# A four-layer graph network on one core: layer rows turned through DRAM in 128-byte pieces, PSUM banks 2/2/4, residual sums in two pieces, and another planned order

## The chip, the cores and the metric

The kernel runs on one core of a Trainium2 chip. The metric is the device time of one execution in microseconds (us), from start to end of the program. A core has five engines with queues of their own: PE (TensorE, matrix products), DVE (VectorE), ACT (ScalarE), POOL (GpSimd) and SP (SyncE, which issues nearly all DMAs here). PE writes only to PSUM, a memory of eight banks of 512 fp32 numbers per partition; DVE and ACT empty the banks.

## The reference, cut to what matters

The input is x, 128 graphs of 64 nodes with 256 features, and an integer adjacency matrix per graph. Four layers follow each other; each normalizes the rows, cuts negatives to zero, computes something over the graph, and adds it to x (the residual sum).

```
h = maximum(layernorm(x), 0);  x = x + elu(attention_4_heads(h, adj))
h = maximum(layernorm(x), 0);  x = x + elu(attention_1_head(h, adj))
h = maximum(layernorm(x), 0);  x = x + relu(relational_conv(h, adj))
h = maximum(layernorm(x), 0);  x = x + gru_3_steps(h, adj)
# one gru step:  m = h @ weight[i];  a = A^T @ m;  h = gru_cell(a, h)
```

All is fp32. An adjacency entry above 1 or very large attention scores would take a general path that is built into the program and is skipped for these inputs.

## The kernel before, in words

**Tiling.** The 8192 rows are cut into 16 groups of 512 rows (`G` = 4 tiles of 128 partitions). Each group passes layer 0, layer 1, layer 2 (called "the layers" here) and then three recurrent steps. A step is 42 matrix products of 256 columns (six sets of seven products in a scheme that saves one product in eight; the sums of weights are prepared in `wsum`, the sums of states on POOL in `hS` and `aS`). The steps of two neighbouring groups are interleaved: (1,0), (0,2), (1,1), (2,0), ... The layers of later groups are filled in between.

**Rows to columns.** A layer needs its normalized rows `hn` turned, with features on the partitions (`hT`), because PE contracts over partitions. For groups from 2 on `layernorm_T_by_dma` does this without PE. ACT writes `hn`; DVE turns 32x32 blocks into `tb` (same buffers as `hn`); one DMA writes all of `tb` to the DRAM tile `way`, in pieces of 4 KB; four DMAs read it back into `land`, in pieces of 1 KB; two ACT copies `hT<-hn` (the profile calls `land` by its buffer, `hn`) bring the pieces into the order that the products want. The recurrence turns its rows in a like manner (`way<-tb`, then `hnat<-way` or `hT<-way`), and is not changed.

**PSUM.** `Banks.room` splits the eight banks: three for `mt` (shared by all tiles of the layers and of the adjacency products, `mm`, `mn`, `tp`, `tq`), two for `sy` and three for `sz`, which take the products of the recurrent steps. A tile takes a free bank of its kind; its first product waits until the last reader of the bank's former tile is done.

**Small products.** `along` (states times adjacency), `aggregate_graphs` and the last product of layer 2 use 64x64 quarters of PE. `beside` (line 842) issues each such block of products as one unit, so no other product stands inside it. There are 130 such blocks.

**Residual sums.** `elu_add` (layers 0 and 1, from group 1 on) and `Recurrence.finish` add a group's result to `xg` in one POOL instruction over 128x1024 numbers.

**Who sets the order.** No engine's order follows the source. Every call is recorded as an `Op`; `Plan.emit` then simulates the engines with estimated durations (`cost`, `port`), 40 times forward and backward from a random start (`SEED`), takes the best ranks, shifts the jobs' due times by a fixed list of pseudo-random moves (`MOVES`), and emits all instructions in the resulting order, engine by engine. All instructions so emitted carry line 550 in the profile, so tiles tell them apart. In the first 115 us, where the plan sees PE idle, it puts in products of a constant (`warm`, line 1664; into an `sz` bank, read by nobody).

```
PASSES, SEED, SPREAD = 40, 35, 50.0
ISSUE, TURN = 665.0, 197.0
took -= self.TURN if op.parts and parts else 0.0     # one small block right after another
```

Of the kernel before, what the change touches and what calls it, by code (L numbers as in the profile page):

```python
# [10 lines left out]
F32 = mybir.dt.float32  # L11
# [6 lines left out]
S = 32  # L18
# [204 lines left out]
class Plan:  # L223
# [30 lines left out]
    def note(self, engine, call, cost, writes, reads, after=(), port=0.0, dma=False):  # L254
# [23 lines left out]
            b.ops.append(op)  # L278
        return op

    PASSES, SEED, SPREAD = 40, 35, 50.0
    MOVES = (
        10, 23, 28, 30, 40, 45, 69, 85, 99, 108, 114, 116, 126, 132, 141, 159, 210, 227, 236, 241, 319, 326, 339, 343,
        354, 365, 383, 426, 448, 489, 544, 596, 636, 646, 651, 652, 704, 736, 741, 742, 743, 752, 760, 807, 869, 944,
        951, 987, 991, 1089, 1101, 1110, 1124, 1248, 1251, 1273, 1452, 1492, 1498, 1501, 1678, 1834, 1893, 1966, 2005,
        2010, 2196, 2270, 2336, 2377, 2433, 2441, 2584, 2658, 2695, 2697, 2873, 3006, 3016, 3031, 3058, 3081, 3167,
        3224, 3271, 3376, 3444, 3459, 3524, 3571, 3664, 3704, 3719, 3750, 3772, 3786, 3953, 4165, 4169, 4192, 4344,
        4481, 4581, 4610, 4913, 4970, 5115, 5123, 5266, 5287, 5433, 5732, 6133, 6139, 6156, 6871, 6933, 7088, 7813,
        7842, 8883, 9045, 9231, 9268, 10172, 10189, 10284, 10634, 10814, 10991, 13029, 13068, 13352, 13896, 14140,
        16577, 16772, 17027, 533, 1980, 2724, 3643, 4767, 7708,  # L290
    )
    LEEWAY = {"PE": 100.0, "DVE": 100.0, "Activation": 100.0, "Pool": 100.0, "SP": 300.0, "-": 0.0}
    OVERLAP = {"DVE": 83.0, "Activation": 95.0, "Pool": 43.0}
# [318 lines left out]
def kernel(  # L612
# [122 lines left out]
    def layernorm_T_by_dma(work, dram, src, hT, natural=None):  # L735


        n = src.shape[1]
        st = work.tile([P, n, 6], F32, name="st")
        mv = work.tile([P, n, 2], F32, name="mv")  # L740
        for p in range(n):
            nc.vector.bn_stats(st[:, p, :], src[:, p, :])
            nc.vector.bn_aggr(mv[:, p, :], st[:, p, :])
        var = work.tile([P, n], F32, name="var")
        rstd = work.tile([P, n], F32, name="rstd")
        nm = work.tile([P, n], F32, name="nm")
        nc.scalar.activation(var, mv[:, :, 1], AF.Identity, bias=eps)
        nc.scalar.mul(nm, mv[:, :, 0], -1.0)
        nc.gpsimd.tensor_tensor(rstd, var, mhalf[:, :n], ALU.pow)
        nc.gpsimd.tensor_tensor(nm, nm, rstd, ALU.mult)  # L750
        hn = work.tile([P, n, D], F32, name="hn") if natural is None else natural
        for p in range(n):
            to, of = hn[:, p], src[:, p, :]
            if natural is not None:
                to, of = spread(hn[:, :, p : p + 1]), of.rearrange("p (k i b) -> p k i b", k=K, b=S)
            nc.scalar.activation(to, of, AF.Relu, bias=nm[:, p : p + 1], scale=rstd[:, p : p + 1])
        if natural is not None and hT.shape[1] == K:
            tb = work.tile([P, K, n, P], F32, name="tb")
            for k in range(K):
                nc.vector.transpose(  # L760
                    tb[:, k].rearrange("p n (j b) -> p n j b", b=S),
                    hn[:, :, :, k * S : (k + 1) * S].rearrange("p j n b -> p n j b"),
                )
            for i in range(P // S):
                for j in range(P // S):
                    to = hT[j * S : (j + 1) * S].rearrange("p k n (i c) -> p (k n) i c", c=S)[:, :, i]
                    of = tb[i * S : (i + 1) * S].rearrange("p k n q -> p (k n) q")
                    nc.sync.dma_start(to, of[:, :, j * S : (j + 1) * S])
            return
        if natural is not None:  # L770
            tb = work.tile([P, P // S, K, n, S], F32, name="tb")
            for k in range(K):
                nc.vector.transpose(
                    tb[:, :, k].rearrange("p j n c -> p n j c"),
                    hn[:, :, :, k * S : (k + 1) * S].rearrange("p j n b -> p n j b"),
                )
            way = dram.tile([P, P // S, K * n * S], F32, name="way")
            nc.sync.dma_start(way, tb.rearrange("p j k n c -> p j (k n c)"))
            for j in range(P // S):
                nc.sync.dma_start(  # L780
                    hT[j * S : (j + 1) * S].rearrange("p i k x -> p i (k x)"),
                    way[:, j].rearrange("(i b) x -> b i x", b=S),
                )
            return
        tb = work.tile([P, P // S, K, n, S], F32, name="tb")
        nc.vector.transpose(
            tb.rearrange("p j k n c -> p n k j c"), hn.rearrange("p n (k j b) -> p n k j b", k=K, b=S)
        )
        way = dram.tile([P, P // S, K * n * S], F32, name="way")
        nc.sync.dma_start(way, tb.rearrange("p j k n c -> p j (k n c)"))  # L790
        land = work.tile([P, P // S, K * n, S], F32, name="land")
        for j in range(P // S):
            nc.sync.dma_start(
                land[j * S : (j + 1) * S].rearrange("p i x c -> p i (x c)"),
                way[:, j].rearrange("(i b) x -> b i x", b=S),
            )
        for a in range(2):
            nc.scalar.copy(
                hT[:, a].rearrange("p k n (e c) -> p (k n) e c", c=S),
                land[:, 2 * a : 2 * a + 2].rearrange("p e x c -> p x e c"),  # L800
            )

    def transpose_blocks(psum, dst, src, rblocks, scale=1.0, turned=False):
# [46 lines left out]
    def elu_add(work, src, o, engine, by_scalar=False):  # L850

        em = work.tile(list(o.shape), F32, name="em")
        if by_scalar:
            nc.scalar.activation(em, o, AF.Relu, scale=-1.0)
            nc.scalar.activation(em, em, AF.Exp, scale=-1.0)
        else:
            nc.vector.tensor_scalar(em, o, 0.0, None, op0=ALU.min)
            nc.scalar.activation(em, em, AF.Exp)
        nc.vector.scalar_tensor_tensor(em, em, -1.0, o, op0=ALU.add, op1=ALU.max)
        engine.tensor_tensor(src, src, em, ALU.add)  # L860

    def block_diagonal(dst, src, scalar, op):

# [116 lines left out]
    class Recurrence:  # L980
# [72 lines left out]

        def finish(self):

            to = self.src.rearrange("p n (k i b) -> p (n k) i b", k=K, b=S)
            nc.gpsimd.tensor_tensor(to, to, spread(self.hnat), ALU.add)
            self.store(self.src, slice(None))

        def step(self, i, back=True, in_parts=False):  # L1060
# [159 lines left out]
    with ExitStack() as s1:  # L1220
# [4 lines left out]
        class Banks(Pool):  # L1225
# [4 lines left out]
            early = psum = spare = True  # L1230

            def room(self, tag, base):
                return {"mt": 3, "sy": 2, "sz": 3}.get(tag, 1)


            def tile(self, shape, dtype, name, **kwargs):
# [31 lines left out]
        class Layer:  # L1268

            place = {"em": "hn", "dg": "hn", "tb": "hn", "land": "hn"}

            shared = {"hn": 3, "o": 2, "st": 4, "mv": 4, "var": 4, "rstd": 4, "nm": 4, "rec": 4}

# [384 lines left out]
        if 115.0:  # L1660
            warm = const.tile([P, P], F32, name="warm")
            nc.nc.vector.memset(warm, 1.0)
            pause = psum.real.tile([P, P], F32, name="sz", tag="sz", bufs=3)
            nc.spare = lambda: psum.spare and nc.nc.tensor.matmul(pause, warm, warm, start=True, stop=True)  # L1664
        with tc.manual_schedule(engines={getattr(mybir.EngineType, e) for e in ENGINES.values()}):
            nc.emit()
# [215 lines left out]
```

## Time and profile before

| | us |
|---|---|
| three runs | 1311.43, 1312.52, 1318.44 (median 1312.52) |
| profiled execution, device time | 1311.0 |
| its span, first to last instruction | 1309.2 |
| PE busy | 1288.8 (98% of the span) |
| DVE, ACT, POOL busy | 1052.5, 857.7, 700.3 |
| mean busy share of the 16 DMA engines | 35% |
| granted PE clock | 0.997 of full |

The profiled execution is 1.5 us below the median. Outside its span lie 1.8 us. A busy PE is not a full one: matrix products are pipelined, their records overlap and their ends are modelled, so a short wait can hide within "busy". Where it matters, the distance of two starts in the timeline is read instead. In a row of a group, "out<-in" are the program's tiles, then partitions x elements; for a product the stationary operand's name may stand first.

### The profile page before, as it was taken

The page shows a single profiled execution, that of the slowest core. Times are in us where ns is not written, and L with a number is a line of the kernel's source. Part 1 is how long each engine was busy: PE and PEld are TensorE (multiplying, and loading weights), DVE is VectorE, ACT ScalarE, POOL GpSimd, SP SyncE. Part 2 cuts the span into 40 slices and gives each one's busy share as a digit, 9 for nine tenths or more (in the row PEclk, how much of TensorE's full clock was granted, in tenths as well). Part 3 has the DMA queues.
Part 4 walks back from the last instruction along what each step waited for, and adds up shares of the span by engine and source line. Part 5 has one row for each costly group of instructions (what it writes and reads, how often), then busy time and mean ns, then how long its engine had stood idle before and what let it go on. Part 6 is the DMA issues. An engine that isn't in the chain of part 4 may idle for free.

```text
span 1309.2 us, 27708 instructions
## 1 busy us (share of the span) xinstructions
PE 1288.8 (98%) x9761; PEld 1024.4 (78%) x9761; DVE 1052.5 (80%) x2532; ACT 857.7 (66%) x2179; POOL 700.3 (53%) x859
## 2 busy tenths in 40 slices
PE   9999999999999999999999999999999999999996
PEld 8667877788777887777787787778878787778885
DVE  7887788968879798887968879796969877776665
ACT  7876666766667676666657657766766667655543
POOL 4845454645555473655527456373747556435443
PEclk9999999999999999999999999999999999999998
DMA  8202133343343434334333444433334433322112
GB/s 249 87 19 63 33 118 106 112 128 118 118 125 111 141 98 135 131 104 122 128 112 114 121 136 122 130 130 102 118 98 138 146 86 117 104 77 71 60 65 69
DMA packets 139349, 142.64 MB, mean 109 GB/s; under 512 B 46912, under 2 KB 126272, under 8 KB 139200
## 3 DMA queue, kind: packets, MB, share of 16 engines
q1 hardware_dynamic: 137856, 140.50, 35.1%
q8 instruction: 80, 1.31, 0.4%
q14 instruction: 69, 0.57, 0.1%
q10 hardware_dynamic: 1344, 0.27, 0.1%
HBM read 78.39 MB, written 61.80 MB: 107 GB/s over the span
## 4 chain that ended last, share of the span: by engine, by line
PE 86%; DVE 6%; POOL 3%; ACT 3%; issue 1%; DMA 1%; SPq 0%; DVEq 0%; ACTq 0%; POOLq 0%
PE sy L550 35%; PE sz L550 26%; PE mm L550 16%; PE mm L842 3%; PE tp L842 3%; DVE hT L550 2%; DVE t L550 1%; PE tp L550 1%; POOL rstd L550 1%; ACT hn L550 1%; PE sz L1664 1%; PE tq L842 1%; POOL xg L550 1%; DVE r L550 1%; DMA t<-row 1%
## 5 line engine op out<-in xcount | busy, mean ns | idle before, releaser
L550 POOL TENSOR_TENSOR r<-hT,hT 128x256 f32<-128x256 f32 x192 | 154.4, 811 | 237.7 <-ACT hT L550 236.9
L550 DVE SCALAR_TENSOR_TENSOR hT<-r,hT 128x256 f32<-128x256 f32 (+1 forms) x290 | 186.4, 647 | 27.1 <-ACT r L550 24.7
L550 PE MATMUL sy<-aS,wsum 128*128 128x256 f32 x576 | 172.8, 384 | 1.9 <-DVE hT L550 1.9
L550 PE MATMUL sy<-hS,wsum 128*128 128x256 f32 x576 | 171.2, 383 | 2.0 <-ACT z L550 1.5
L550 PE MATMUL sz<-hS,whh 128*128 128x256 f32 x576 | 171.4, 383 | 0.6 <-DVE z L550 0.5
L550 PE MATMUL sz<-aS,wc 128*128 128x256 f32 x576 | 164.9, 382 | 0.9 <-DVE hT L550 0.9
L550 DVE TENSOR_TENSOR hT<-hT,sz 128x256 f32<-128x256 f32 x288 | 117.7, 410 | 42.6 <-PE sz L550 38.9
L550 ACT ACTIVATE hT<-hT,bi 128x256 f32<-128x256 f32 x192 | 95.8, 504 | 51.8 <-DVE hT L550 51.3
L550 PEld LDWEIGHTS sy<-hS,wsum 128*128 128x128 f32 x576 | 107.1, 190 | 27.8 <-issue 5.9
L550 POOL TENSOR_TENSOR rstd<-var,mhalf 128x4 f32<-128x4 f32 (+1 forms) x70 | 76.7, 1095 | 97.2 <-ACT var L550 92.5
L550 PEld LDWEIGHTS sy<-aS,wsum 128*128 128x128 f32 x576 | 107.2, 190 | 25.1 <-issue 6.0
L550 PEld LDWEIGHTS sz<-aS,wc 128*128 128x128 f32 x576 | 108.2, 190 | 21.6 <-issue 5.8
L550 PEld LDWEIGHTS sz<-hS,whh 128*128 128x128 f32 x576 | 107.5, 190 | 21.9 <-issue 5.9
L550 ACT ACTIVATE hT<-sy,bh 128x256 f32<-128x256 f32 x192 | 90.0, 469 | 49.8 <-PE sy L550 48.6
L550 POOL TENSOR_TENSOR aS<-aT 128x256 f32<-128x256 f32 x96 | 79.0, 823 | 81.6 <-ACT aT L550 78.8
L550 PE MATMUL mm<-wl,hT 128*128 128x512 f32 x248 | 118.9, 595 | 1.3 <-DVE u L550 1.0
L550 ACT ACTIVATE hn<-xg,nm,rstd 128x256 f32<-128x256 f32 x200 | 109.4, 594 | 15.1 <-POOL nm L550 11.9
L550 ACT COPY z<-sy 128x256 f32<-128x256 f32 x192 | 70.2, 369 | 66.8 <-PE sy L550 65.2
L550 DVE TENSOR_TENSOR hT<-hT,sy 128x256 f32<-128x256 f32 x192 | 79.2, 412 | 37.5 <-PE sy L550 35.1
L550 DVE TENSOR_TENSOR z<-sz,z 128x256 f32<-128x256 f32 x192 | 79.6, 416 | 25.7 <-PE sz L550 23.4
L550 DVE BATCH_NORM_STATS2 st<-xg 128x6 f32<-128x256 f32 x256 | 95.6, 406 | 5.1 <-DMA xg<-in_x_dram 3.1
L550 POOL TENSOR_TENSOR hS<-hT 128x256 f32<-128x256 f32 x96 | 81.8, 852 | 24.5 <-DVE hT L550 15.2
(212 smaller groups left out, 3197.9 us busy)
## 6 DMA issues: line engine op xcount, KB each, us to landing
way<-tb SPq DMA_DIRECT2D x59, 512.0 KB, 2.7
hnat<-way SPq DMA_DIRECT2D x184, 128.0 KB, 3.0
way<-hn SPq DMA_DIRECT2D x42, 512.0 KB, 3.0
hn<-way SPq DMA_DIRECT2D x168, 128.0 KB, 2.9
xg<-in_x_dram SPq DMA_DIRECT2D x15, 512.0 KB, 4.3
out_dram<-xg SPq DMA_DIRECT2D x15, 512.0 KB, 3.0
t<-row SPq DMA_DIRECT2D x28, 256.0 KB, 4.0
hT<-way SPq DMA_DIRECT2D x52, 128.0 KB, 2.9
```

The costliest lines, as they stand in the source:

```text
L550: return do(*[real(a) for a in args], **{k: real(v) for k, v in kwargs.items()})
L842: nc.nc.tensor.matmul(*[real(x) for x in product], start=True, stop=True)
L1664: nc.spare = lambda: psum.spare and nc.nc.tensor.matmul(pause, warm, warm, start=True, stop=True)
```

## The change

Five edits, in one diff:

1. **Turned rows.** `way` and `land` are replaced by a DRAM tile `fine`. Four DMAs write `tb` (one for each 32 partitions, pieces of 1 KB), and two DMAs, one for each half `e`, read 256 KB each straight into `hT`, in 128-byte pieces. The two ACT copies are gone, and `land` no longer takes an `hn` buffer. This is done 42 times.
2. **Banks.** `mt` 3 to 4, `sz` 3 to 2, `sy` stays 2.
3. **`elu_add`** adds in two instructions over half the tiles each.
4. **`finish`** likewise.
5. **`SEED` 35 to 36 and a new list `MOVES`**: all engines' orders change.

```
-    PASSES, SEED, SPREAD = 40, 35, 50.0
+    PASSES, SEED, SPREAD = 40, 36, 50.0
     MOVES = (
-        10, 23, 28, 30, 40, 45, 69, 85, 99, 108, 114, 116, 126, 132, 141, 159, 210, 227, 236, 241, 319, 326, 339, 343,
...
+        4, 9, 10, 16, 23, 24, 27, 52, 54, 69, 126, 127, 131, 135, 153, 160, 168, 195, 197, 225, 228, 230, 231, 238,
...
     )
...
-        way = dram.tile([P, P // S, K * n * S], F32, name="way")
-        nc.sync.dma_start(way, tb.rearrange("p j k n c -> p j (k n c)"))
-        land = work.tile([P, P // S, K * n, S], F32, name="land")
-        for j in range(P // S):
+        fine = dram.tile([2, P // S, S, 2, K * n * S], F32, name="fine")
+        for i in range(P // S):
             nc.sync.dma_start(
-                land[j * S : (j + 1) * S].rearrange("p i x c -> p i (x c)"),
-                way[:, j].rearrange("(i b) x -> b i x", b=S),
+                fine[i % 2, :, :, i // 2].rearrange("j b x -> b j x"),
+                tb[i * S : (i + 1) * S].rearrange("p j k n c -> p j (k n c)"),
             )
-        for a in range(2):
-            nc.scalar.copy(
-                hT[:, a].rearrange("p k n (e c) -> p (k n) e c", c=S),
-                land[:, 2 * a : 2 * a + 2].rearrange("p e x c -> p x e c"),
+        for e in range(2):
+            nc.sync.dma_start(
+                hT.rearrange("p a k n (e c) -> p (a k n) e c", c=S)[:, :, e],
+                fine[e].rearrange("j b a (x c) -> (j b) (a x) c", c=S),
             )
...
-        engine.tensor_tensor(src, src, em, ALU.add)
+        n = src.shape[1]
+        m = max(1, n // 2)
+        for p in range(0, n, m):
+            engine.tensor_tensor(src[:, p : p + m], src[:, p : p + m], em[:, p : p + m], ALU.add)
...
-            to = self.src.rearrange("p n (k i b) -> p (n k) i b", k=K, b=S)
-            nc.gpsimd.tensor_tensor(to, to, spread(self.hnat), ALU.add)
+            m = G // 2
+            for p in range(0, G, m):
+                to = self.src[:, p : p + m].rearrange("p n (k i b) -> p (n k) i b", k=K, b=S)
+                nc.gpsimd.tensor_tensor(to, to, spread(self.hnat[:, :, p : p + m]), ALU.add)
...
-                return {"mt": 3, "sy": 2, "sz": 3}.get(tag, 1)
+                return {"mt": 4, "sy": 2, "sz": 2}.get(tag, 1)
...
-            place = {"em": "hn", "dg": "hn", "tb": "hn", "land": "hn"}
+            place = {"em": "hn", "dg": "hn", "tb": "hn"}
...
-            pause = psum.real.tile([P, P], F32, name="sz", tag="sz", bufs=3)
+            pause = psum.real.tile([P, P], F32, name="sz", tag="sz", bufs=2)
```

## The prediction

> **What bounds the kernel now.** I read the page's busy shares first, then its chain of waits, then PE's timeline, measuring each wait as the distance between starts less the products' own time.
>
> ```profile
> PE 1288.8 (98%) x9761; PEld 1024.4 (78%) x9761; DVE 1052.5 (80%) x2532; ACT 857.7 (66%) x2179; POOL 700.3 (53%) x859
> ...
> PE 86%; DVE 6%; POOL 3%; ACT 3%; issue 1%; DMA 1%; SPq 0%; DVEq 0%; ACTq 0%; POOLq 0%
> ```
>
> PE sets the end: nothing else is near 98%, and the chain is 86% PE. No edit removes a needed product, so only what keeps PE from its products can change. By the timeline (a 256-column product starts 0.43 us after the one before) that is:
> - start-up, to 95 us: 11 gaps over 0.25 us, 5.9 us in all, beside 48 `warm` products of 0.22 us (10.5 us);
> - 95 to 1250 us: nine gaps, 8.9 us in all: 0.43 (at 217), 0.89 (220), 1.64 (386), 1.82 (526), 1.38 (600), 1.18 (639), 0.42 (1027), 0.44 (1111), 0.68 (1140);
> - the end, from 1290 us: six gaps, 4.5 us, and 7.7 us from the last product to the end of the output DMA;
> - the edges of 130 small blocks.
>
> The edges, in PE's timeline (start, duration, operation):
>
> ```profile
> 631.91 0.59 PE L550 MATMUL sy<-hS,wsum 128*128 128x256 f32 x2
> 632.44 0.27 PE L842 MATMUL tp<-abd,hnat 64*64 64x64 f32 x2
> 632.45 0.27 PE L842 MATMUL tq<-abd,hnat 64*64 64x64 f32 x2
> 632.54 0.23 PE L842 MATMUL tp<-abd,hnat 64*64 64x64 f32 x2
> ...
> 633.38 0.23 PE L842 MATMUL tq<-abd,hnat 64*64 64x64 f32 x2
> 633.53 0.70 PE L550 MATMUL sy<-aS,wsum 128*128 128x256 f32 x2
> ```
>
> The large product ends its turn at 632.34 and the next starts at 633.53: 1.19 us. Inside, 16 rounds follow each other by 0.058 us: 0.93 us. So 0.26 us of a block is edge.
>
> The largest kind of gap, in the timeline of all engines:
>
> ```profile
> 383.75 2.80 POOL L550 TENSOR_TENSOR xg<-xg,hn 128x1024 f32<-128x1024 f32 x1
> ...
> 384.60 2.50 DVE L550 SCALAR_TENSOR_TENSOR hT<-r,hT 128x512 f32<-128x512 f32 x1
> ...
> 385.83 0.59 PE L550 MATMUL sz<-hS,whh 128*128 128x256 f32 x2
> ...
> 387.20 0.37 ACT L550 COPY r<-sy 128x256 f32<-128x256 f32 x1 [1.99 <-DVE hT L550]
> ...
> 387.47 0.38 ACT L550 COPY z<-sy 128x256 f32<-128x256 f32 x1
> ...
> 387.90 0.70 PE L550 MATMUL sy<-hS,wsum 128*128 128x256 f32 x2 [1.48 <-ACT z L550]
> ```
>
> A POOL residual sum runs; the DVE operation beside it, about 0.7 us otherwise, ends only 0.6 us after POOL does; ACT waits for DVE, so empties an `sy` bank late; PE waits 1.64 us for the bank. The gaps at 217, 220 and 526 fall beside a residual sum in the same way, and the one at 639 behind a DVE operation that waited for it: 5.96 of the 8.9 us.
>
> **What the Trainium skill says.**
> - *SBUF — State Buffer*, "Who interferes with whom": a DVE instruction with two SBUF inputs and a GpSimd instruction that reads SBUF exclude each other for a whole instruction. The trace agrees: 2.50 us above.
> - *TensorEngine Tiling (Array Packing)*, "Key Properties": changing the tiling mode drains TensorE. The trace agrees: 0.26 us a block.
> - *DMA: Bandwidth & Descriptors*, "Why small descriptors are slow (HBM only)": each packet has a fixed overhead. The trace before has no 128-byte reads from DRAM; its nearest rows are below.
>
> **The change part by part.** Beside durations I use the instruction order of the two built programs.
>
> *Order on PE.* Before, each of the 130 small blocks stands alone. After, 97 do, 15 pairs and one triple follow each other directly: 113 runs, 17 fewer pairs of edges. No adjacent blocks are in the trace, so a join saves between 0 and 0.24 us; I take 0.20, as both blocks use the same quarters: 17 x 0.20 = **-3.4** (0 to -4.1).
>
> *Start-up.* 35 `warm` products instead of 48; 72.3 us of other products stand ahead of the first recurrent one in both. 13 x 0.22 = 2.8 us less filler, which ends PE sooner only where what PE then needs is there: I take half, **-1.4** (-5 to +3; the start-up's order is new, and DVE is busy in all of 20 to 40 us).
>
> *Residual sums.* The tile's durations:
>
> ```profile
> L550 POOL TENSOR_TENSOR xg<-xg,hn x32: 1269/2360/2806, 42.9 to 1130.1; 128x1024 f32<-128x1024 f32 x28, 128x512 f32<-128x512 f32 x4
> ```
>
> 47 become 94 (28 and 15 of 1024 numbers become halves of 1.27 us, four of 512 become quarters); 43 x (2 x 1.27 - 2.36) = 8 us more on POOL, covered by its 47% idle. The longest block on DVE falls by 1.09 us: the gaps beside residual sums shrink from 0.43, 0.89, 1.64, 1.82, 1.18 to 0, 0, 0.55, 0.73, 0.09: -4.6 us, if DVE gets in between the halves. Group 0's four sums on DVE become eight.
>
> *Banks.* I summed the products' times between the last product into a tile and the first product of the tile that takes its bank (oldest first). An emptying needs about 0.9 us, so below 1.35 us there is little to spare. Such reuses: before 11 (`mt`), 55 (`sy`), 7 (`sz`); after 0, 60, 46. Six of the nine gaps stand before a product into an `sy` bank: 5.9 us for 55 tight reuses. With halves 3.3 of that goes; 2.6 stays. After has 106 tight reuses of `sy` and `sz`: 2.6 x 106/55 = 5.0 us. The three gaps of layer products (1.38, 1.18, 0.42) become about 1.5. Steady part together: 5.0 + 1.5 - 8.9 = **-2.4** (-7 to +6).
>
> *Turned rows.* ACT loses 84 copies:
>
> ```profile
> L550 ACT COPY hT<-hn 128x512 f32<-128x512 f32 x84 | 49.3, 613 | 5.4 <-DMA hn<-way 4.9 <-issue 0.5
> ```
>
> 49.3 us of an engine at 66%: off PE's path but for the gap of 0.68 us at 1140, where a copy stood behind long ACT work. I count nothing. The DMAs (tile, count, KB each, us to landing), then two stretches whose last columns are DMA share and GB/s:
>
> ```profile
> way<-hn SPq DMA_DIRECT2D x42, 512.0 KB, 3.0
> ...
> hn<-way SPq DMA_DIRECT2D x168, 128.0 KB, 2.9
> ...
> hT<-tb SPq DMA_DIRECT2D x16, 32.0 KB, 2.0
> ```
>
> ```profile
> 1184.00:1194.00 10.00, 10.00 (x48) 8.81 (x47) 5.84 (x14) 4.23 (x10) 0.69 (x2) 1.00 0.28 43
> ```
>
> ```profile
> 349.60:353.00 3.40, 3.40 (x18) 2.97 (x17) 3.38 (x11) 3.12 (x8) 2.74 (x4) 1.00 0.13 29
> ```
>
> The first holds the 16 `hT<-tb` alone, 4096 packets of 128 bytes between SBUF tiles: 0.28 x 10 x 16 / 4096 = 11 ns each. The second holds four `eg` loads, 384 packets of 256 bytes from DRAM and few others: 0.132 x 3.4 x 16 / 438 = 16 ns. A new read has 2048 packets over 16 engines: 128 x 11 to 16 ns = 1.4 to 2.1 us. 84 of them are 118 to 176 us of all engines; the writes and reads they replace nearly cancel (same bytes), so the share goes from 35% to 44-48%: no bound. Path before: write 3.0, issue of four reads 4 x 0.43, landing 2.9, two copies 1.2 = 8.8 us. After: four writes 1.7, landing 2.9, two reads issued at 0.61 each, data 2 x (1.4 to 2.1), about 2 fixed = 10.6 to 12.0, less whatever the issues overlap: 0 to 3 us later. SP issues 252 DMAs instead of 210: 42 x (4 x 0.43 + 2 x 0.61 - 0.34 - 4 x 0.43) = 37 us more of a mostly waiting queue; behind a read that waits for its four writes stand `row<-fT`, `t<-row` and `way<-tb` of the recurrence. Before, PE waits for such rows once (0.42 us at 1027), so most of the delay is covered by the lead of the layers; I take **+0.7** (-0.4 to +20).
>
> *The end.* 19.8 us of products stand after the last adjacency block instead of 17.2, and the first of them to use its result comes 3.4 us after it instead of 1.7: **0** (-1.7 to +1.5).
>
> Sum: -3.4 - 1.4 - 2.4 + 0.7 = -6.5 us on 1311.0: 1304.5 for a profiled execution; the median stood 1.5 above it: **1306.0**.
>
> **The rivals.**
> - *Likeliest (0.52)*: as summed, 1302 to 1309. About two thirds of it lie below the bound of 0.5% (6.6 us, about what a measurement of this kernel can tell from no change), 1305.9.
> - *All gaps close (0.13)*: joins full, steady gaps gone, start-up gains: -4 - 8.5 - 3 = 1297. For it: the order is new everywhere; against: 106 tight reuses.
> - *Nothing that matters (0.20)*: joined blocks still pay their edges, and two `sz` banks cost what halved sums give: +1 to -2, 1310 to 1314.
> - *Slower (0.15)*: the layers' rows land too late. Place: the first product `mm<-w0e`, `mm<-w1e` or `mm<-wl` of each of 42 turns. Price: up to 3 us each, more if a 2048-packet read takes long to issue. With half of them late by 1.3 us: +27 - 6 = 1333; it decides from a mean of 0.32 us per turn ((6.6 + 7) / 42). For it: the DMA path loses its slack while SP gets more to issue; against: PE waited for it once.
>
> **How the numbers follow.** Faster by over 0.5%: 0.35 + 0.13 = 0.48. Within: 0.17 + 0.17 = 0.34, and 0.02 of the last case: 0.36. Slower: 0.13 and 0.03 of the third: 0.16. The range, 1296 to 1320, takes in the second case and the milder half of the last.
>
> **What would show it.** In PE's order in the trace, joined small blocks with under 0.1 us between them; nowhere a DVE operation of 2 us or more beside `xg`; gaps of PE from 95 to 1250 us of 5 to 8 us; `hT<-fine` landing in 4 to 5 us, DMA share near 45%; ACT near 808 us. Wrong would be: PE gaps of over 0.25 us before products into `sz` that sum to over 5 us, layer products waiting for `hT<-fine` more than a few times, or joined blocks as far apart as lone ones.

## The result, and the profile after

| | before | after |
|---|---|---|
| median of ten runs each, us | 1312.84 | 1309.19 |
| all runs, us | 1310.8 to 1318.4 | 1306.7 to 1311.5 |
| profiled execution, its span, us | 1311.0, 1309.2 | 1310.1, 1308.2 |

The ratio is 0.9971 (95% interval 0.9958 to 0.9983): 3.7 us faster, less than the 0.5% that was set as the bound. In a later group of runs on another occasion it was 0.9961 (0.9944 to 0.9977). The two profiled executions differ by only 1 us, because before's lies near the lower end of its runs: in four groups of runs before took 1309.9 to 1319.1 us, with medians of 1312.8, 1313.0, 1314.0 and 1315.6. Between the first and the last product of the recurrence pass 1202.6 us in the trace before and 1203.1 in the trace after: in these two executions all that is gained lies in the start-up. What before loses in its longer runs no kept trace shows.

The page of the kernel after, busy times and the chain of waits (PE's share of the chain was 86%):

```profile
PE 1289.3 (99%) x9735; PEld 1022.2 (78%) x9735; DVE 1051.5 (80%) x2536; ACT 817.6 (63%) x2095; POOL 708.1 (54%) x906
...
PE 69%; DVE 12%; DMA 6%; ACT 4%; POOL 4%; issue 2%; SPq 2%; ACTq 0%; DVEq 0%; POOLq 0%
```

PE still sets the end, but the chain now passes more often through another engine: DVE 12% instead of 6%, DMA 6% instead of 1%. POOL has 8 us more, ACT 40 us less.

PE's timeline of the kernel after, at a place where a block of `tp`/`tq` products is followed by one of `mm`/`mn` (start, duration, operation):

```profile
126.43 0.23 PE L841 MATMUL tp<-abd,hnat 64*64 64x64 f32 x2
126.44 0.22 PE L841 MATMUL tq<-abd,hnat 64*64 64x64 f32 x2
126.49 0.22 PE L841 MATMUL tp<-abd,hnat 64*64 64x64 f32 x2
126.50 0.23 PE L841 MATMUL tq<-abd,hnat 64*64 64x64 f32 x2
126.54 0.23 PE L841 MATMUL mm<-wh,t 64*64 64x65 f32 x2
126.56 0.23 PE L841 MATMUL mn<-wh,t 64*64 64x65 f32 x2
...
126.97 0.22 PE L841 MATMUL mn<-wh,t 64*64 64x65 f32 x2
127.12 0.70 PE L551 MATMUL sy<-hS,wsum 128*128 128x256 f32 x2
```

From 126.49 to 126.54 there is no edge: the second block starts one round after the last of the first. At the end stands the usual edge, 126.97 to 127.12. Joined blocks pay one pair of edges, as forecast.

The durations of the tile `xg` in the kernel after (count, then min/median/max in ns), and those of `hT` on DVE:

```profile
L551 POOL TENSOR_TENSOR xg<-xg,hn x64: 722/1270/2312, 43.2 to 1137.1; 128x512 f32<-128x512 f32 x56, 128x256 f32<-128x256 f32 x8
```

```profile
L551 DVE SCALAR_TENSOR_TENSOR hT<-r,hT x290: 375/426/1397, 100.7 to 1299.8; 128x256 f32<-128x256 f32 x96, 128x512 f32<-128x512 f32 x49
```

The longest `hT<-r,hT` on DVE was 2575 ns before. Over the whole trace seven DVE operations took 1.9 us or more before, none does after. Part of the cost has moved: two POOL halves take 2.3 us instead of 1.27, both beside a `hn<-hn,o` that started on DVE within 0.03 us of them.

The DMAs of the turned rows (tile, count, KB each, us to landing):

```profile
fine<-hn SPq DMA_DIRECT2D x168, 128.0 KB, 2.3
hT<-fine SPq DMA_DIRECT2D x84, 256.0 KB, 4.0
```

What PE waits for in the kernel after (us in total, times, longest), of which these bear on the change:

```profile
PE sy L551 <- DMA hnat<-way: 2.2, 1, 2.2
PE sz L551 <- DVE z L551: 1.4, 4, 0.7
...
PE mm L551 <- DMA hT<-fine: 0.4, 1, 0.4
```

By the distances in PE's timeline, the gaps over 0.25 us between 95 and 1250 us are 10.9 us in 20 (before: 8.9 in nine): 4.35 us in ten before products into `sz` (before, none of this kind stood among the nine), 5.7 us in eight before products into `sy`, 0.8 us before layer products. Of the `sy` part, 3.8 us are one cluster at 1194 to 1202 us:

```profile
1194.78 0.70 PE L551 MATMUL sz<-aS,wc 128*128 128x256 f32 x2
1197.63 1.58 PE L551 MATMUL sy<-hT,whh 128*128 128x256 f32 x4 [2.15 <-DMA hnat<-way]
1199.01 1.06 PE L551 MATMUL sy<-aT,wc 128*128 128x256 f32 x2
1199.86 1.85 PE L551 MATMUL sz<-hT,whh 128*128 128x256 f32 x4
```

Only the first 2.4 us of the cluster are a wait. Behind it the products follow each other at half speed, 0.43 us from record to record instead of 0.216 (a product is two records), and for that the profile shows no wait: PE's granted clock was halved for 3.41 us from 1198.1 us on (window, its length, PE busy and instructions, granted clock, DMA share, GB/s):

```profile
1198.10:1201.50 3.40, 3.40 (x9) 0.50 0.01 2
1201.60:1205.00 3.40, 3.40 (x75) 1.00 0.02 5
```

Half of 3.41 us is 1.7 us of lost work. The trace before has no such stretch ahead of its last recurrent product.

An example of the `sz` kind, in the timeline of all engines of the kernel after:

```profile
907.61 0.59 PE L551 MATMUL sy<-aS,wsum 128*128 128x256 f32 x2
...
908.06 0.43 DVE L551 TENSOR_TENSOR t<-t,gd 128x256 f32<-128x256 f32 x1 [1.56 <-DMA t<-row]
...
908.40 0.42 DVE L551 TENSOR_TENSOR z<-sz,z 128x256 f32<-128x256 f32 x1
...
908.87 0.70 PE L551 MATMUL sz<-hS,whh 128*128 128x256 f32 x2 [0.67 <-DVE z L551]
```

DVE takes its operations in order. It stood 1.56 us at a `t` whose rows had not come; behind it stood the operation that empties an `sz` bank, and with two such banks PE lost 0.83 us.

### The profile page after: what moved, and what is told of

It is laid out like the page before. It is cut to its first block, busy times and chain, and to the rows that moved or that the text cites. A ratio compares the mean times of both kernels' runs of the same rounds, so it can differ in the third digit from the quotient of the medians.

```text
span 1308.2 us, 27536 instructions
## 1 busy us (share of the span) xinstructions
PE 1289.3 (99%) x9735; PEld 1022.2 (78%) x9735; DVE 1051.5 (80%) x2536; ACT 817.6 (63%) x2095; POOL 708.1 (54%) x906
## 4 chain that ended last, share of the span: by engine, by line
PE 69%; DVE 12%; DMA 6%; ACT 4%; POOL 4%; issue 2%; SPq 2%; ACTq 0%; DVEq 0%; POOLq 0%
PE sy L551 28%; PE sz L551 21%; PE mm L551 14%; DVE hT L551 3%; PE mm L841 3%; PE tp L841 2%; DVE t L551 2%; ACT hn L551 2%; SPq L551 2%; DMA t<-row 2%; DVE r L551 1%; POOL xg L551 1%; DMA row<-fT 1%; DVE tb L551 1%; DVE st L551 1%
## 5 line engine op out<-in xcount | busy, mean ns | idle before, releaser
L551 DVE SCALAR_TENSOR_TENSOR hT<-r,hT 128x256 f32<-128x256 f32 (+1 forms) x290 | 174.9, 610 | 25.3 <-ACT r L551 23.6
L551 PE MATMUL sz<-aS,wc 128*128 128x256 f32 x576 | 170.2, 384 | 0.0
L551 POOL TENSOR_TENSOR rstd<-var,mhalf 128x4 f32<-128x4 f32 (+1 forms) x70 | 79.7, 1139 | 58.9 <-ACT var L551 50.5
L551 DVE SCALAR_TENSOR_TENSOR r<-z,r 128x512 f32<-128x512 f32 (+1 forms) x98 | 86.4, 887 | 10.8 <-POOL r L551 8.6
```

What stands on the lines that cost most here:

```text
L551: return do(*[real(a) for a in args], **{k: real(v) for k, v in kwargs.items()})
```

## The experiments

The difficulty is the planner: an edit that changes a recorded operation gives another order of everything, and the lists of moves were found for one structure each. So most kernels here **keep the planned order**: they change what an operation emits when its turn comes, and leave what the planner sees. Four others have an order of their own, and tell how far orders differ by themselves. Ratios are to before on the same chip, with 95% intervals; us are that difference times before's median in that group.

### Residual sums whole again, in after's order

```
-            engine.tensor_tensor(src[:, p : p + m], src[:, p : p + m], em[:, p : p + m], ALU.add)
+            # planned as before in two pieces; the first emits the whole sum, the second nothing
+            noted(engine, (lambda: add(engine, src, em)) if p == 0 else lambda: None,
+                  src[:, p : p + m], em[:, p : p + m])
```

(`finish` likewise.)

> The kernel after with every instruction in the same order on every engine, but each residual sum as one operation again (the first half's place does the whole sum, the second half's place nothing). Theory A (the halves are what shortens the DVE operations beside them, and PE's waits with them): DVE operations of over 2 us beside `xg` come back, PE's gaps over 0.25 us between 95 and 1250 us grow by 4 to 8 us from 10.9, and the time by 3 to 7 us against the kernel after (1312 to 1316). Theory B (the gain is the new order's, whatever the sums): within 1 us of the kernel after. Theory C (two more semaphore waits and 43 more POOL operations cost what the halves bring): faster than the kernel after by 1 to 3 us.

Measured: 1330.21 us, ratio 1.0113 (1.0095 to 1.0131); the kernel after would be at 0.997, so about 19 us slower than it. Its tile `xg`, and two of PE's waits:

```profile
L858 POOL TENSOR_TENSOR xg<-xg,hn x32: 1264/2355/3391, 42.7 to 1154.5; 128x1024 f32<-128x1024 f32 x28, 128x512 f32<-128x512 f32 x4
```

```profile
PE sz L551 <- DVE z L551: 7.0, 9, 2.0
PE sz L551 <- DVE hT L551: 2.5, 7, 0.6
```

15 DVE operations take 1.9 us or more, PE's gaps between 95 and 1250 us grow from 10.9 to 25.1 us (39 gaps), and the first recurrent product starts 1 us later. Theory A in kind, about three times as much in size: after's order was laid around halves, and with two `sz` banks late operations of DVE reach PE (its waits for `DVE z` before `sz` go from 1.4 to 7.0 us). The traces agree with the size: the last recurrent product comes 18.1 us later. A whole sum costs far more in this order than in the one that was planned with it.

### Residual sums in halves, in before's order

```
-        engine.tensor_tensor(src, src, em, ALU.add)
+        def emit():
+            for p in range(0, n, m):
+                add(engine, src[:, p : p + m], em[:, p : p + m])
+
+        noted(engine, emit, src, em)        # planned as one
```

> The kernel before with every instruction in the same order, but each residual sum as two operations of half the size, one directly behind the other on POOL (or DVE for group 0). Theory A, by the prediction's own working: the gaps beside residual sums shrink by 4.6 us, so 4.6 us faster than before (about 1308; 3 to 6 us). Theory B (the gain is the new order's): within 1 us of before. Theory C: where DVE does not get in between two operations that stand directly behind each other on POOL, long DVE operations stay at 2.5 us and nothing is gained, or 1 us lost.

Measured: 1312.09 us, ratio 0.9968 (0.9957 to 0.9979): 4.2 us faster than before. No DVE operation reaches 1.9 us; the longest `hT<-r,hT` is 1499 ns. Theory C falls: DVE does get in between two sums that stand directly behind each other. By the medians theory A holds, and one edit of five brings about what the change as a whole brings. The size is less sure than the interval says, as before's median was higher on this occasion (1315.6 us) than on the others (1312.8 to 1314.0).

Place by place the trace bears the working out only in part. Of the five gaps that were to shrink or go, those at 220 and 386 us do (0.89 to nothing over 0.25, 1.64 to 0.58), but those at 217, 526 and 639 stay (0.42, 1.71 and 1.16). The sum and DVE at 524:

```profile
523.58 2.83 POOL L859 TENSOR_TENSOR xg<-xg,hnat 128x512 f32<-128x512 f32 x2 [2.27 <-DMA hnat<-way]
523.80 2.90 DVE L550 SCALAR_TENSOR_TENSOR hT<-r,hT 128x256 f32<-128x256 f32 x2
```

Here two `hT<-r,hT` follow each other on DVE, and each ends just behind one half of the sum (1.50 and 1.48 us; before 2.58 and 0.41). The first is shorter, the pair is not. The trace also has gaps that before's has not (1.2 us at 920, 1.6 at 936), and its last recurrent product comes 2.6 us later than in before's trace. So the shorter DVE operations are shown, and the gain by the medians; at which gaps the gain is made is not.

### Joined blocks taken apart

The list that is to be emitted is changed: where a small block follows another on PE, the next large product goes in between (15 of 17 places; at the other two that product is itself a small block, depends on the block or on its bank, or stands in the start-up).

```
+            if not (pe[n - 1][0].parts and pe[n][0].parts):
+                continue
...
+            listed.insert(i, listed.pop(j))
```

> The kernel after, every engine but PE in the same order; on PE, 15 of the 17 places where one block of small products directly follows another are undone by moving the next large product in between. Theory A (a joined block saves its pair of edges, 0.22 us by the two traces): 15 x 0.22 = 3.3 us slower than the kernel after (2 to 4.5, some of it lost in waits that PE has anyway). Theory B (PE is not held to its products there, or the edges are paid anyway): within 1 us.

Measured: 1313.25 us, ratio 0.9982 (0.9974 to 0.9990). Against the kernel after's 0.9971 and 0.9961 that is 1.4 to 2.8 us slower, and the intervals overlap a little. PE's timeline of this kernel at the place shown above:

```profile
126.40 0.22 PE L858 MATMUL tp<-abd,hnat 64*64 64x64 f32 x2
126.41 0.23 PE L858 MATMUL tq<-abd,hnat 64*64 64x64 f32 x2
126.57 0.70 PE L568 MATMUL sy<-hS,wsum 128*128 128x256 f32 x2
127.20 0.27 PE L858 MATMUL mm<-wh,t 64*64 64x65 f32 x1
```

The large product takes 0.43 us; from 126.41 to 127.20 pass 0.79. Both edges are back. At places without another wait, each undone join puts all that follows 0.35 us later in the trace (the block itself runs 0.04 us longer beside its 0.30 us of edges); at 1150 us the sum is 4.5 us, at the end 4.3. The medians taken directly (1313.25 against 1309.19 and 1309.43) differ by about 4 us; the ratios give less, because before's median was highest on this occasion. Theory A, at its full size or a little more.

### Reads of 2 KB instead of 128 bytes

```
-                hT.rearrange("p a k n (e c) -> p (a k n) e c", c=S)[:, :, e],
-                fine[e].rearrange("j b a (x c) -> (j b) (a x) c", c=S),
+                hT.rearrange("p a k n x -> p (a k n x)")[:, e * K * n * N : (e + 1) * K * n * N],
+                fine[e].rearrange("j b a x -> (j b) a x").rearrange("q a x -> q (a x)"),
```

> The kernel after with every instruction in the same order, but `hT<-fine` reads the same bytes in pieces of 2 KB to the partition's own place instead of 128-byte pieces (the rows land in wrong places, so the rearrangement is left out and the result is other numbers). Theory A (the small pieces cost nothing on PE's path, their landing is covered): DMA share falls from 44% to 33 to 37%, `hT<-fine` lands in 2.5 to 3.2 us instead of 4.0, time within 1 us of the kernel after. Theory B (late rows or busy DMA engines cost part of what the rest gains): 2 to 4 us faster than the kernel after, with fewer gaps of PE before layer products and fewer waits for `hnat<-way`, whose landing was slower in the kernel after.

Measured: 1307.8 us, ratio 0.9941 (0.9928 to 0.9954): 2.6 to 3.9 us faster than the kernel after. DMA share 37.4%, and from its DMA issues:

```profile
hT<-fine SPq DMA_DIRECT2D x84, 256.0 KB, 3.4
```

Theory B by the time, but not by its way: the gaps before layer products stay (0.8 us in two). At 1194 us PE stands level with the kernel after beside the others (next section), ten us later it is 2.2 us ahead:

```profile
1194.24 0.70 PE L551 MATMUL sz<-aS,wc 128*128 128x256 f32 x2
1196.60 1.10 PE L551 MATMUL sy<-hT,whh 128*128 128x256 f32 x4 [1.66 <-ACT z L551]
...
1201.31 0.70 PE L551 MATMUL sy<-hS,wsum 128*128 128x256 f32 x2
```

The last `hT<-tb` land 0.5 us earlier, so PE's wait is 1.9 us instead of 2.4, and its releaser is now `ACT z`; and the clock is not halved behind it, which is 1.7 us. Up to there the 0.6 us of landing, 84 times, bring nothing on balance. So what the small pieces cost in this order is, in these traces, that one wait and what follows from it.

### The kernel after beside the others

> The kernel after, unchanged, beside the other kernels of this group on one chip, so that differences of 0.2% between them can be read. Ratio to before 0.996 to 0.998, as at first.

Measured: 1309.43 us, ratio 0.9961 (0.9944 to 0.9977); gaps of 10.8 us in 19 between 95 and 1250 us, the first recurrent product at 93.2 us (93.3 in the first trace). The place of the section above, in this trace:

```profile
1194.22 0.70 PE L551 MATMUL sz<-aS,wc 128*128 128x256 f32 x2
1197.13 1.98 PE L551 MATMUL sy<-hT,whh 128*128 128x256 f32 x4 [2.21 <-DMA hnat<-way]
...
1203.53 0.70 PE L551 MATMUL sy<-hS,wsum 128*128 128x256 f32 x2
```

The clock is halved here too, for 3.41 us from 1197.2 us on. Whether it is may change from one execution to the next: of the seven runs, four have a mean granted clock of 0.996 and took 1309.4 to 1310.4 us, three have 0.997 and took 1307.7 to 1308.6. That fits a stretch of 3.41 us at half clock (0.0013 of the span); which of the unprofiled runs had it is not shown. The six runs with 2-KB reads, all at 0.997 or 0.998, took 1307.2 to 1308.9 us, much as these three.

### Half of 16 DMAs from ACT's queue

```
-                    nc.sync.dma_start(to, of[:, :, j * S : (j + 1) * S])
+                    queue = ("sync", "scalar")[j % 2]      # planned on SP, in the same order
```

> The kernel after in the same order, but of the 16 `hT<-tb` DMAs near 1184 us every second one is issued by ACT's queue instead of SP's. Theory A (PE's stall of 2.4 us at 1194 and those of 0.5 and 0.8 behind it come from SP issuing 16 DMAs one after the other for 10.6 us): the stall goes, 2 to 3.7 us faster than the kernel after. Theory B (the stall is of something else that is late there, or ACT, which issues for some 5 us in the middle of its work, holds PE up elsewhere): within 1 us, with a gap of about the same size near 1190 to 1200.

Measured: 1308.07 us, ratio 0.9953 (0.9935 to 0.9971), within the uncertainty of the kernel after. The stall stays, 2.35 us at 1194.7:

```profile
PE sy L551 <- DMA hT<-tb: 2.1, 1, 2.1
```

The test was too weak: ACT has its instructions in order too, the DMAs stood between its planned operations, and the last was issued at 1193.8 us, as late as from SP. But the releaser's name is now `hT<-tb`, so it is these rows that are late, and with the 2-KB reads PE waits there for `ACT z` instead. Two waits stand behind each other at this place; taking away the first would leave some 1.9 us.

The trace also prices the halved clock. The wait is nearly as long as in the kernel after (2.35 and 2.4 us), but the clock stays full behind it:

```profile
1197.60:1201.00 3.40, 3.40 (x16) 1.00 0.00 0
```

Up to this wait the trace stands 0.1 us ahead of the first trace of the kernel after, at 1204 us 1.8.

### Small pieces in the write instead of the read

```
+            of = real(tb)[i * S : (i + 1) * S].rearrange("p j k n c -> p (j k n) c")
+            to = place()[i // 2, :, :, :, i % 2].rearrange("b j x c -> b (j x) c")     # 128-byte pieces
...
+                    place()[a].rearrange("b j x e c -> j b (x e c)"),                  # 2-KB pieces
```

> The kernel after in the same order and with the same result, but the 128-byte pieces stand in the write `fine<-hn` instead of the read `hT<-fine`, which becomes two reads in 2-KB pieces behind the fourth write. Theory A (what 128-byte pieces cost is the late landing of the read on the rows' path, or other transfers behind it): reads land in 2.3 to 3 us, 1 to 4 us faster than the kernel after. Theory B (they cost what they take of the DMA engines, wherever they stand): DMA share stays at 42 to 46%, time within 1 us. Theory C (small writes take longer than small reads): slower by 1 to 4 us, with `hnat<-way` and `t<-row` landing later than 3.7 us.

Measured: 1349.97 us, ratio 1.0261 (1.0238 to 1.0284): 40 us slower than the kernel after. Its tile `fine` and PE's waits:

```profile
L801 SPq DMA_DIRECT2D fine<-hn x168: 550/667/3335, 32.1 to 1192.7; - x168
...
  PE mm L551: 20.7, 17
```

Theory C, ten times its size. Three things are mixed in it: the issue of a write takes 667 ns instead of 434, and both reads now stand behind the fourth write, where in the kernel after each read needs only two of the four; and the clock was halved six times, 30.7 us in all, so up to 15 us of the 40 are the halved clock. The DMA share is 39.7%, below the kernel after's 44.0%: the share does not show this cost, the wait of layer products for `hT<-fine` does, 20.7 us in 17 times where it was 0.4 us once. This is what the "slower" rival of the prediction feared.

### The new way of turning rows, in before's order

The four writes are emitted at the place of the `way` write, the two reads behind the four `land` reads (or behind the last reader of the `hT` buffer, where that is later), and nothing for the two ACT copies:

```
-            nc.scalar.copy(hT[:, a]..., land[:, 2 * a : 2 * a + 2]...)
+            op = nc.note("Activation", lambda: None, cost("scalar", "copy", (to, of), {}), [to], [of])
+            op.taken, op.read = reads, lambda: (read(0), read(1))
```

> The kernel before with every instruction in the same order, but the turned rows of the layers by four `fine` writes at the place of the `way` write, two 128-byte reads behind the place of the four `land` reads, and without ACT's 84 copies. Theory A, the prediction's own term: 0.7 us slower than before (-0.4 to +3), ACT at 808 us. Theory B (as the kernel with 2-KB reads makes likely): the small pieces cost 2 to 5 us, through rows that land late and other transfers behind them: 1315 to 1318 where before is 1313. Theory C (the 49 us that ACT loses empty banks earlier): 1 to 4 us faster than before.

Measured: 1319.45 us, ratio 1.0041 (1.0029 to 1.0052): 5.4 us slower than before. Its tile is still called `way`; PE's waits, and the landing of the reads:

```profile
PE mm L566 <- DMA hT<-way: 3.5, 5, 2.1
```

```profile
hT<-way SPq DMA_DIRECT2D x84, 256.0 KB, 4.9
```

Theory B. Layer products wait five times for the turned rows, up to 2.1 us, and the gaps between 95 and 1250 us grow to 17.2 us. ACT falls to 817 us; the time shows no gain from it. In this order, which was planned with the old way, the edit is a plain loss. Part of it may come from where the reads are issued, behind the places of the old ones; and they land in 4.9 us instead of the 4.0 of the kernel after.

### Banks 3, 2, 3 with an order of their own

```
-                return {"mt": 4, "sy": 2, "sz": 2}.get(tag, 1)
+                return {"mt": 3, "sy": 2, "sz": 3}.get(tag, 1)
...     # and a new list MOVES
```

> The kernel after with banks 3, 2, 3 as before, and an order searched anew for it by the same planner (SEED 36 and moves of its own; its planned end is 1294.3 us, the kernel after's 1292.5). No two blocks of small products follow each other in its order (each block holds two `mt` banks, so two in a row need four). Theory A (the fourth `mt` bank is worth the 17 joins, 3.7 us, and the third `sz` bank the gaps before `sz` products, 4.4 us; they cancel): gaps of PE before `sz` products fall below 1 us, time within 2 us of the kernel after. Theory B (two `sz` banks cost more than the joins bring): 3 to 5 us faster than the kernel after. Theory C (the joins count, the `sz` banks don't): 4 to 7 us slower.

Measured: 1318.57 us, ratio 1.0044 (1.0028 to 1.0061): some 10 us slower than the kernel after. PE's timeline has the first recurrent product here:

```profile
97.55 0.70 PE L552 MATMUL sy<-hT,whh 128*128 128x256 f32 x2
```

That is 4.2 us later than in the kernel after. 16 joins fewer are 3.5 us, and the gaps between 95 and 1250 us are 14.6 us instead of 10.9: before `sz` products three are left (3.2 us) of ten, but before `sy` products 15 stand, 9.4 us. One of the three, 2.45 us at 1038, is followed by a halved clock (1.7 us). Nearest to theory C, and beyond its 4 to 7 us; but a start-up that is 4 us worse is an order's doing, and only the joins follow from the banks: a block holds two `mt` banks. What the fourth `mt` bank does can be seen in the orders: those with three `mt` banks (before and three kernels here) have at most one joined pair, the two with four have 17 and 15 joins.

### Halves planned in, everything else as before

```
+        for p in range(0, n, m):
+            engine.tensor_tensor(src[:, p : p + m], src[:, p : p + m], em[:, p : p + m], ALU.add)
...     # and a new list MOVES
```

> The kernel before with the halved residual sums in the plan and an order searched for it (planned end 1294.4 us, before's 1292.9); banks 3, 2, 3 and the old way of turning rows. Theory A (halves bring what they brought in the old order, 4.2 us, and the plan's 1.5 us more are real): 2.7 us faster than before, ratio 0.998. Theory B (planned in, the halves bring more, since POOL and DVE can be laid around them): 5 us or more, ratio 0.996 or below, as fast as the kernel after. Theory C (the order decides, not the halves): as before or slower.

Measured: 1310.0 us, ratio 0.9978 (0.9968 to 0.9988): 2.9 us faster than before. Theory A: the halves' 4.2 us less the 1.5 us by which this plan is longer. No DVE operation of 1.9 us, gaps of 7.8 us in 14, one joined pair.

### The old way of turning rows, the rest as after

```
-        fine = dram.tile([2, P // S, S, 2, K * n * S], F32, name="fine")
+        way = dram.tile([P, P // S, K * n * S], F32, name="way")
...     # land and the two copies as before, and a new list MOVES
```

> The kernel after with the old way of turning rows (`way`, `land`, two ACT copies), banks 2, 2, 4 and halved sums, and an order searched for it, less far than the others (planned end 1297.3 us, 4.8 above the kernel after's). Theory A (128-byte pieces cost what they cost in the two orders, 3 to 5 us, and that is all that `fine` does): plan and pieces cancel, within 2 us of the kernel after. Theory B (the new way of turning rows gains by what it takes off ACT): 4 to 8 us slower than the kernel after. Theory C (the pieces cost more than that): 2 us or more faster than the kernel after although its plan is longer.

Measured: 1311.49 us, ratio 0.9985 (0.9976 to 0.9995): 1.8 to 3.2 us slower than the kernel after (the intervals overlap), on a plan that is 4.8 us longer. It lies at the edge of theory A; that the new way's cost, 2 to 3 us, hides in the difference is not shown. That reading rests on planned microseconds being real ones, which the run before bears out (1.5 planned, 1.3 measured) and the one with banks 3, 2, 3 does not (1.8 planned, 10 measured).

### Another order for before

```
     # 32 more moves, planned end 1293.2 instead of 1292.9 us; nothing else
```

> The kernel before with another order from the same planner: its own list of moves and 32 more, taken so that the planned end stays within 0.3 us of before's (1293.2 to 1292.9 us). Nothing else differs. Theory A (orders that are planned equally long run equally long): ratio to before 0.999 to 1.001. Theory B (the order by itself moves the time by as much as the change did): over 3 us from before, to either side, with PE gaps at other places; then the gain of the change can't be told from a lucky order by its time alone.

Measured: 1311.69 us, ratio 0.9993 (0.9980 to 1.0005). Theory A: an order that is planned as long, and stays near before's, runs as long, within 0.2%. This one other order does not bring the change's gain; how far such orders spread, one of them cannot tell.

## Why the prediction was right, and where its sum was not

The forecast was 1306.0 us with a range of 1296 to 1320; 1309.19 came, 3.2 us above the point and 0.2 above the likeliest case's own range, 1302 to 1309. Of the three outcomes, "within 0.5%" had 0.36 and came; "faster" had 0.48. For a profiled execution 1304.5 was forecast, and the two took 1310.1 and 1309.4: there the miss is 5 to 5.6 us. The median came nearer only because it lies 0.9 us below the first profiled execution, where 1.5 above had been reckoned. Point by point:

- **What bounds the kernel: right.** PE is busy for 98 and 99% of the span. What tells these kernels apart is PE's gaps and edges, and in some the halved clock, which the prediction did not have.
- **Joined blocks, -3.4: right in kind and near in size.** In the two traces, PE's time at edges falls by 4.4 us, of which 1.2 come back as steps inside the joined blocks: -3.1. Taking 15 of 17 apart costs 1.4 to 2.8 us by the ratios and about 4 by the traces and medians. *TensorEngine Tiling (Array Packing)*, "Key Properties", of the Trainium skill, on the drain at a change of the tiling mode, is borne out: a join of two blocks of different shapes (64x64, then 64x65) on the same quarters has none.
- **Start-up, -1.4: right, somewhat small.** The first recurrent product starts at 93.3 us instead of 95.3; four more runs in after's order had it at 92.9 to 93.3, and two in before's at 95.9 and 96.4.
- **Residual sums, -4.6: right in kind; the size is not settled.** -4.2 by itself in before's order, by medians; in the trace two of five gaps shrink. It rests on *SBUF — State Buffer*, "Who interferes with whom": a DVE instruction with two SBUF inputs and a POOL instruction that reads SBUF exclude each other for a whole instruction. The traces agree: with whole sums seven, eight, nine and 15 DVE operations take 1.9 us or more; with halved ones none in five kernels, and one or two in four, all `hn<-hn,o`. Not all have two SBUF inputs: `abd<-at`, 2.27 us beside a sum in the trace before, has one. What the working left out is that two such DVE operations in a row can each wait for one half.
- **Gates' and layers' gaps, 5.0 + 1.5 us: mis-sized, the largest miss.** 10.9 us came, outside the 5 to 8 that were to show it. The ten `sz` gaps (4.35 us) are what the 46 tight reuses were taken to bring, and stay below the 5 us that would have been "wrong". What was not seen is the cluster of 3.8 us at 1194 us: 2.4 us of wait, where the new order puts the products on `hT` right behind 16 serial `hT<-tb` DMAs that both kernels have (before ran other products there), and the rest halved clock. The count of tight bank reuses looks at PE's order and banks alone, and could not show a product that stands too early behind a DMA. The gaps before layer products came to 0.8 us. The sum itself has a slip: the gaps before `sy` lose 3.5 us by the figures given, not 3.3, and the 5.0 should be 4.6.
- **Turned rows, +0.7: near in the order that was planned for them, wrong in before's.** In after's order layer products wait for the rows once, 0.4 us, so "most of its delay is covered by the lead of the layers" held. By the ratios the 128-byte pieces cost 2.6 to 3.9 us there; by the traces 0.5 us of a wait, not before a layer but before the recurrence at 1194 us, and 1.7 us of halved clock behind it. In before's order the edit costs 5.4 us: five waits came up where the lead had been judged by one of 0.42 us. Landing (4.0 us) and DMA share (44.0%) came as worked out. *DMA: Bandwidth & Descriptors*, "Why small descriptors are slow (HBM only)", has a fixed overhead for each packet, and is borne out in kind: 256 KB land in 4.0 us in 128-byte pieces and in 3.4 us in 2-KB pieces.
- **ACT near 808: 817.6.** An engine's busy time counts overlapping instructions once. The 84 copies are busy for 49.3 us as a group, but overlap with ACT's other instructions at their ends, and only 40.0 us went. It bore on nothing.
- **POOL +8 us: right** (700.3 to 708.1). **The end, 0:** from the last recurrent product to the end of the span 11.1 us became 11.5; the gaps over 0.25 us from 1250 us on fell from 4.5 to 3.4.
- **The rivals.** "Nothing that matters" was half true: two `sz` banks did cost about what halved sums give (4.35 us of gaps), but joined blocks did not pay their edges. "Slower" was the right fear: the mechanism is real, 5.4 us in before's order and 40 us where the small pieces stand in the writes; after's order, planned with it, keeps most of it off PE.

The parts that were measured alone, -4.2 (halves) and +5.4 (turned rows), with the two read from the traces, -3.1 (joins) and -1.9 (start-up), sum to -3.8 us; the medians give -3.7. That they add up so well is luck: the sum leaves out the `sz` gaps and the stretch at 1194 us, and the same edit costs 5.4 or about 3 us, the same halving brings 4.2 or 19, depending on the order around it.

**What stays open.** What two `sz` banks cost apart from the order. Where before loses time in its longer runs. Whether the 3.8 us at 1194 us can be had: issuing all 16 DMAs ahead of ACT's other work was not tried. What halves the clock: small writes apart, five traces have one such stretch, behind waits of 2.1 to 2.5 us; but waits of 2.3 us (half of the DMAs from ACT's queue; the new way in before's order) have none behind them, nor has one of 2.9 us at 1200 us in the kernel with the old way of turning rows. The length of the wait alone does not decide it. No kernel here beats the kernel after by more than the uncertainty with the same result; the 2-KB reads would, but leave the rearrangement out.

## What to carry to other kernels

Price an edit inside the order in which it will run: a planned order absorbs what it was planned with, and punishes what it was not (whole sums cost 4 us in the one order and 19 in the other). To take a change of many parts to pieces, keep the order and change what is emitted; re-planning each variant mixes in the planner's luck. Where PE has waited for some us, read its granted clock behind the wait as well: distances between products that look like more gaps can be slower products. And look at the spread of the runs before you build a sum on one profiled execution: before's took 1311.0 us where its medians are 1312.8 to 1315.6, so a typical run may have more waits to lose than its trace shows.

## What the runs showed that was not expected

- 128-byte pieces are far worse in writes to DRAM than in reads from it: the same bytes, 4096 small pieces in either case for each turned group, cost 4 us at most in reads and some 40 in writes here, while the DMA share fell from 44.0 to 39.7% (part of the 40 us is that both reads then stand behind the last write, and up to 15 are halved clock).
- The issue of a DMA on SP does not grow with its number of pieces alone: `hT<-fine` with 2048 pieces takes 547 ns, a `fine<-hn` write of 1024 small pieces 667 ns, and one of 128 pieces of 1 KB 434 ns.
- Two kernels with halved sums repeat better than before, which took 1310.3 to 1319.1 us in 32 runs and 1309.9 to 1318.0 in 51: halves in before's order 1309.3 to 1313.8 in 11, halves planned in 1308.4 to 1312.1 in 19. It is no rule: with the old way of turning rows and banks 2, 2, 4 halved sums took 1306.5 to 1313.8 in 22, with banks 3, 2, 3 1315.9 to 1322.6 in eight.
- One wait can cost more than its length: behind the wait of 2.4 us at 1194 us PE's clock was halved for 3.41 us, 1.7 us of work; behind a wait of 2.35 us with full clock those 1.7 us were not lost.
